# Ends of stages in a four-layer token kernel: two last blocks in turns, gathers under the softmax, experts in interleaved steps, stores by group

## The chip, the core and the metric

The kernel runs on one core of a Trainium2 chip. The core has a matrix engine (TensorE, "PE" in the profile, with its weight loads as "PEld"), a vector engine (VectorE, "DVE"), an activation engine (ScalarE, "ACT"), a general engine (GpSimd, "POOL"), an engine that mostly issues transfers (SyncE, "SP"), and 16 DMA engines. Each engine has a queue of its own and executes it in order; engines wait for each other through semaphores. ACT and POOL issue transfers too. The metric is the device time of one execution in microseconds (us); lower is better.

## What is computed

The input is eight images of 56 x 56 pixels with 128 channels. Four layers follow one another: a deformable convolution with an MLP, a whitening, and two token layers, in which an image is a list of 3136 tokens of 128 channels. Only the token layers matter here:

```python
t = t + attn(_ln_t(t))            # layer 2: softmax attention, 8 heads of 16
t = t + ffn(_ln_t(t))             # experts, below
t = t + linear_attn(_ln_t(t))     # layer 3: softmax(q), softmax(k), k^T v, norm
t = t + ffn(_ln_t(t))

logits = einsum('bsd,ed->bse', x, gate_w) + gate_b     # 64 experts
probs = softmax(logits, axis=1)                        # over the tokens
vals, idx = top_k(probs.transpose(0, 2, 1), 8)         # 8 tokens for each expert
pooled = einsum('bked,bke->bed', gathered, topv)       # weighted sum of the 8
h = gelu(einsum('ebd,edh->ebh', [pooled, 1], weight1)) # 512 hidden
out = einsum('ebh,eho->ebo', [h, 1], weight2)
outputs = zeros.at[idx].add(out * topv)                # back to the 8 tokens
```

Each expert chooses its eight tokens in an image by their gate logits, so an image's choice can be made only when all of its logits exist.

## The kernel before

The convolution and the whitening come first and are not touched. `token_layers` then runs these stages, one after another:

1. `attention_keys` normalises the tokens and makes the keys of all images.
2. `attend` is the softmax attention. Its scheduling is written out by hand: every engine runs its instructions in the order of the program. An image has two groups of four heads; a group has eight blocks of queries (384 wide, the last 448) and goes through the key tiles in steps. Scores are products on PE (L1252) into the bank pairs of pool `pss`, exponentials on ACT (L1260), 32 x 32 transposes on DVE (L1271) that let one exponential serve two pairs of blocks, moves of these squares by SP (L1287, twelve transfers a set) and POOL (L1298), and weighted sums on PE (L1305), added by DVE (L1324).
   A finished block goes through `finish`: divide by the sum (L1345 to L1353), load its tokens (L1359), project with p_o (L1366), add to the tokens (L1377), store them to `t_a` (L1378), statistics (L1382 to L1385, the power on POOL), normalise to `xn` (L1392), transpose on PE (p_tr, L1404), copy to `xT` (L1405), gate product (p_g, L1408), and write the logits `pr` (L1409). `finish` is a generator: at each `yield` the main loop takes back control and calls `go_on` once a step at most, the oldest block first. p_o, p_tr, p_g and the running sum `avx` share one bank (pool `psm`, tag `m`), so a `yield True` asks for a step at which that bank is free. When the loop has ended, the blocks that are left are finished one after another.
   After the last block of an image, `choose` (L1643 to L1707) takes the eight largest logits of each expert (MAX8, L1650) and their positions (FIND_INDEX8, L1653), the sum of exponentials (seven pieces on ACT, L1663), spreads positions and weights over 128 partitions by small products with an identity (p_take, L1679), gathers the tokens by indirect transfers of POOL (four, L1711), takes their statistics (L1697), normalises and weighs them and sums them to `pooled` (L1706).
3. `run_experts` makes the experts of layer 2. Two pieces of work alternate: `Spread.prepare` of each image (four gathers, and the matrix `s_w` that takes expert outputs back to tokens: `same` on DVE, L1757, added by POOL, L1767), and `Experts.run`, which goes through the 64 experts in 16 quarters of four. A quarter is: p_h (L1855 and bias L1859), gelu on ACT (L1861), transposes p_ht (L1864), copy to `hT` on DVE (L1868), p_o (L1872 and bias L1880), copy to `o` on DVE (L1883), four stores by ACT (L1887). Its weights, two transfers of 1 MB (L1823, L1826), are loaded four quarters ahead by SP; each quarter issues those of the quarter four later at its end. `Spread.run` then adds the result to the gathered tokens and scatters them back (32 indirect transfers, L1791).
4. `context_sums` makes k^T v of the linear attention.
5. `linear_layer` (L2064 to L2153) handles groups of 448 tokens, seven to an image. The groups run through `pipeline`, which starts one a turn and advances all that are in flight. The tokens of an image lie in one tile; each group adds its result to its part (POOL, L2129) and takes statistics. The last group of an image stores the whole image twice, to `t_c` and to the output (L2138), and goes on with `choose`.
6. `run_experts` again, with the weights of layer 3; its final scatter goes to the output.

Outside `attend` the order of instructions on each engine is decided by a scheduler at build time, from the dependencies and the program's order. Transfers that SP and ACT issue take eight semaphores in rotation, so each of them waits for the one eight places before it.

Of the kernel before, what the change touches and what calls it, by code (L numbers as in the profile page):

```python
# [19 lines left out]
T = 112  # L20
# [1134 lines left out]
def attend(tc, k, w, low, tok, kT_in, va_in, t_out, gate_w, gate_b, taken, pooled):  # L1155
# [11 lines left out]
    with ExitStack() as ctx:  # L1167
# [166 lines left out]

        def finish(n, g, b):
# [27 lines left out]
            p = psm.tile([128, KB + 1, C], F32, tag="m", name="p_o")  # L1363
# [9 lines left out]
            st = wp.tile([128, KB + 1, 6], F32, name="st")  # L1373
            mv = wp.tile([128, KB + 1, 2], F32, name="mv")
            rs = wp.tile([128, KB + 1], F32, name="rs")
# [14 lines left out]
            xn = wp.tile([128, KB + 1, C], F32, name="xn")  # L1390
            for i, (_, m) in enumerate(tiles):
                nc.vector.tensor_scalar(  # L1392
                    xn[:m, i],
                    t_sb[:m, i],
                    mv[:m, i, 0:1],
                    rs[:m, i : i + 1],
                    ALU.subtract,
                    ALU.mult,
                )
            yield True  # L1400
            xT = wp.tile([C, QB + 64], F32, name="xT")
            p = psm.tile([C, 512], F32, tag="m", name="p_tr")
            for i, (_, m) in enumerate(tiles):
                nc.tensor.transpose(p[:, 128 * i : 128 * i + m], xn[:m, i], k.ident[:m, :m])  # L1404
            nc.vector.tensor_copy(xT[:, :width], p[:, :width])  # L1405
            yield True
            p = psm.tile([E, 512], F32, tag="m", name="p_g")
# [15 lines left out]
        ready = []  # L1423
# [61 lines left out]
        for work in urgent:  # L1485
            go_on(work)
        while later:
            go_on(later[0])
# [156 lines left out]
def choose(nc, k, wp, ps, pr, t_in, taken, pooled):  # L1645
# [12 lines left out]
    nc.scalar.activation(found[:, 1], best, AF.Exp, bias=ntop)  # L1658
    yield
# [17 lines left out]
    p = ps.tile([128, 2, NC], F32, tag="m", name="p_take")  # L1677
    for j in range(TOP // NC):
        nc.tensor.matmul(  # L1679
            p[E * j : E * j + E],  # L1680
            k.ident[:E, :E],
            found[:, :, j :: TOP // NC],
            start=True,
            stop=True,
        )
    rows = wp.tile([128, NC], I32, name="rows")
    nc.vector.tensor_copy(rows, p[:, 0])
    nc.vector.tensor_copy(taken, p)
    x = wp.tile([128, NC, C], F32, name="chosen")
    for c in range(NC):  # L1690
        gather(nc, x[:, c], t_in, rows[:, c : c + 1])
    for _ in range(4):
        yield
# [107 lines left out]
class Experts:  # L1801

    def __init__(self, tc, pool, weight1, weight2, ahead):
        nc = tc.nc
        self.tc, self.pool = tc, pool
        self.weight1, self.weight2 = weight1, weight2
        self.loaded = [self.load(q) for q in range(ahead)]

        self.b1 = pool.tile([E, HID], F32, name="b1", bufs=1)
        nc.scalar.dma_start(self.b1, weight1[:, C, :])
        self.b2 = pool.tile([E, C], F32, name="b2", bufs=1)
        nc.scalar.dma_start(self.b2, weight2[:, HID, :])

        self.x = pool.tile([C, E, 32], F32, name="x", bufs=1)
        nc.gpsimd.memset(self.x, 0.0)

    def load(self, q):
        nc = self.tc.nc  # L1820
        es = slice(q * EG, (q + 1) * EG)
        w1 = self.pool.tile([C, EG, HID], F32, name="w1")
        nc.sync.dma_start(w1, self.weight1[es, :C, :].rearrange("e d h -> d e h"))  # L1823

        w2 = self.pool.tile([128, EG, 4 * C], F32, name="w2")
        nc.sync.dma_start(  # L1826
            w2, self.weight2[es, :HID, :].rearrange("e (p f) o -> p e (f o)", f=4)
        )
        return w1, w2

    def run(self, k, pooled, out):
# [4 lines left out]
        with ExitStack() as ctx:  # L1836
# [7 lines left out]
            loaded = list(self.loaded)  # L1844
            ahead = len(loaded)
            for q in range(n_q):
                w1, w2 = loaded[q]
                p = ps.tile([128, HID], F32, tag="h", name="p_h")
                rows = [p[32 * j : 32 * j + 32] for j in range(EG)]
                ones = [  # L1850
                    k.ident[:E, e : e + 1].to_broadcast([E, 32])
                    for e in range(q * EG, q * EG + EG)
                ]
                for j in range(EG):
                    nc.tensor.matmul(  # L1855
                        rows[j], x[:, q * EG + j], w1[:, j], start=True, stop=False
                    )
                for j in range(EG):
                    nc.tensor.matmul(rows[j], ones[j], self.b1, start=False, stop=True)  # L1859
                h = wp.tile([128, HID], F32, name="h")  # L1860
                nc.scalar.activation(h, p, AF.Gelu)  # L1861
# [6 lines left out]
                nc.vector.tensor_copy(hT, p)  # L1868
                p = ps.tile([128, C], F32, tag="o", name="p_o")
                for f in range(4):  # L1870
                    for j in range(EG):
# [3 lines left out]
                            w2[:, j, f * C : (f + 1) * C],  # L1875
# [3 lines left out]
                for j in range(EG):  # L1879
                    nc.tensor.matmul(  # L1880
                        p[32 * j : 32 * j + 32], ones[j], self.b2, start=False, stop=True
                    )
                nc.vector.tensor_copy(o[:, q], p)  # L1883
                if q + ahead < n_q:
                    loaded.append(self.load(q + ahead))
                for j in range(EG):
                    nc.scalar.dma_start(out[:, q * EG + j], o[32 * j : 32 * j + n_b, q])  # L1887
                yield
# [174 lines left out]
def linear_layer(tc, k, w, low, cw, t_in, xT_in, t_out, out, gate_w, gate_b, taken, pooled):  # L2063
# [5 lines left out]
    with ExitStack() as ctx:  # L2069
# [5 lines left out]
        def group(n, g):  # L2075
# [60 lines left out]
            if g == NG - 1:  # L2136
                for d in (t_out[n], out[n]):
                    nc.sync.dma_start(d.rearrange("(t p) c -> p t c", p=T), st_of[n][0])  # L2138
# [205 lines left out]
```

## Time and profile before

The median of three runs is 7727.34 us (7716.75 to 7728.98). The profile is that of one execution.

| | us |
|---|---|
| profiled execution | 7718.14 |
| its span, first to last instruction | 7716.3 |
| attention, end of its loop at about | 6500 |
| last logits of attention (end of the `pr` writes) | 6553.6 |
| first experts: first gather | 6582.2 |
| POOL's last addition to `s_w` there | 6655.9 |
| linear layer, about | 7033 to 7451 |
| its last `pooled` | 7481.8 |
| second experts: first gather | 7486.1 |
| final scatter | from 7626 on |

PE is busy 84% of the span, DVE 68%, ACT 54%, POOL 38%. These shares are averages over stages with different limits, so they must be read stage by stage. In a timeline row, the numbers are the start and the duration; then come the engine, the line, the operation, what it writes and reads, and in square brackets how long the engine had been idle and which instruction released it. The granted clock of PE is a share of full speed.

### The profile page before, as it was taken

What the parts mean: (1) busy time and instruction counts of PE and PEld (TensorE: products, weight loads), DVE (VectorE), ACT (ScalarE), POOL (GpSimd) and SP (SyncE); (2) the same over time, 40 slices, a digit from 0 to 9 for tenths busy, and PEclk for the clock granted to TensorE, in tenths of its full rate; (3) what the DMA queues carried; (4) which work ended last, traced back from release to release, by engine and by line L of the source; (5) the groups of instructions that cost most, each with busy time, mean ns of one, the idle gap of its engine ahead of it and who ended that gap; (6) DMA issues with size and microseconds to landing.
All of it is one profiled execution on the core that took longest, in us unless ns stands there. A gap on an engine that the chain in (4) does not pass through costs nothing. (4 is left out here: it accounts for less than half of the span.)

```text
span 7716.3 us, 157926 instructions
## 1 busy us (share of the span) xinstructions
PE 6482.3 (84%) x59883; PEld 2880.7 (37%) x59883; DVE 5284.8 (68%) x9856; ACT 4142.6 (54%) x6467; POOL 2935.1 (38%) x2555
## 2 busy tenths in 40 slices
PE   6659999556899999999999999999999997556654
PEld 4446666334233323323323323333333333245532
DVE  7975564366677777777777777777777776366752
ACT  4424444122666666666666666666666664056740
POOL 0011111022444444444444444444444443434653
PEclk8768898777999999999999999999999998788766
DMA  5453443376788778778778778778778775543543
GB/s 155 137 119 76 86 95 65 82 240 207 199 203 197 193 192 199 189 192 201 191 184 204 188 183 207 183 191 205 185 190 206 182 190 137 196 117 107 134 135 130
DMA packets 736303, 1287.38 MB, mean 167 GB/s; under 512 B 117698, under 2 KB 503108, under 8 KB 728516
## 3 DMA queue, kind: packets, MB, share of 16 engines
q1 hardware_dynamic: 725556, 1260.76, 65.1%
q0 software_dynamic: 6144, 12.60, 0.6%
q8 instruction: 484, 7.93, 0.5%
q10 hardware_dynamic: 3824, 3.68, 0.2%
q14 instruction: 295, 2.42, 0.1%
HBM read 286.04 MB, written 197.81 MB: 63 GB/s over the span
## 5 line engine op out<-in xcount | busy, mean ns | idle before, releaser
L1260 ACT ACTIVATE e<-p_s 128x768 f32<-128x768 f32 (+2 forms) x3712 | 2887.8, 830 | 1584.9 <-PE p_s L1252 1329.8
L1298 POOL COPY x<-sq 32x1152 f32<-32x1152 f32 x1792 | 2059.2, 1149 | 2067.6 <-PE p_s L1252 1330.0
L1271 DVE STREAM_TRANSPOSE sq<-e 128x768 f32<-128x768 f32 x2688 | 2434.5, 950 | 567.3 <-ACT e L1260 312.9
L1252 PE MATMUL p_s<-q,kT 32*128 32x384 f32 (+2 forms) x14848 | 1888.6, 548 | 33.6 <-ACT e L1260 18.6
L1305 PE MATMUL av<-e,va 128*32 128x384 f32 (+2 forms) x14848 | 1645.3, 515 | 30.4 <-DVE acc L1324 20.7
L1305 PE MATMUL avx<-x,va 128*32 128x384 f32 x10752 | 1138.3, 496 | 69.5 <-issue 40.2
L1252 PEld LDWEIGHTS p_s<-q,kT 32*128 32x128 f32 (+1 forms) x14848 | 654.8, 181 | 1252.6 <-issue 825.4
L1305 PEld LDWEIGHTS av<-e,va 128*32 128x32 f32 (+1 forms) x14848 | 294.5, 108 | 1049.4 <-issue 941.7
L1305 PEld LDWEIGHTS avx<-x,va 128*32 128x32 f32 x10752 | 353.2, 111 | 650.9 <-issue 595.2
L609 POOL TENSOR_TENSOR rs<-rs,mhalf 112x4 f32<-112x4 f32 x112 | 116.1, 1036 | 788.3 <-DVE rs L608 788.3
L1324 DVE TENSOR_TENSOR acc<-acc,avx 128x384 f32<-128x384 f32 x336 | 183.9, 547 | 229.9 <-PE avx L1305 228.6
L121 PE MATMUL p_tr<-ident,xn 112*128 112x112 f32 x672 | 134.6, 341 | 187.4 <-DVE xn L112 141.8
L1141 POOL TENSOR_TENSOR rs<-rs,mhalf 112x4 f32<-112x4 f32 (+2 forms) x136 | 168.1, 1236 | 269.3 <-DVE ntop L1942 123.8
L525 ACT COPY wT<-p_w 88x448 f32<-88x448 f32 x152 | 138.0, 922 | 194.1 <-PE p_w L523 161.4
L1990 ACT ACTIVATE xn<-t,ms,rs 112x128 f32<-112x128 f32 x448 | 185.3, 488 | 76.4 <-DVE ms L1983 76.4
L327 DVE SCALAR_TENSOR_TENSOR acc<-xp,dw,acc 128x3136 f32<-128x3136 f32 x56 | 194.3, 3478 | 31.3 <-ACT acc L322 31.2
L637 PE MATMUL p_f<-x1T,w 128*128 128x448 f32 x448 | 205.6, 583 | 4.4 <-DVE x1T L632 2.7
L121 PEld LDWEIGHTS p_tr<-ident,xn 112*128 112x128 f32 x672 | 98.7, 169 | 285.0 <-issue 185.1
L1385 POOL TENSOR_TENSOR rs<-rs,mhalf 128x3 f32<-128x3 f32 (+1 forms) x72 | 58.5, 815 | 365.0 <-DVE rs L1384 343.0
L523 PE MATMUL p_w<-ident,wide 112*88 112x112 f32 x896 | 146.5, 303 | 58.6 <-DMA px<-strips 34.1
L621 DVE TENSOR_TENSOR y<-y,p_rs 128x448 f32<-128x448 f32 x112 | 69.3, 619 | 176.6 <-PE p_rs L614 176.6
L122 ACT COPY xT<-p_tr 128x448 f32<-128x448 f32 x112 | 59.6, 532 | 229.8 <-PE p_tr L121 203.7
(354 smaller groups left out, 7830.9 us busy)
## 6 DMA issues: line engine op xcount, KB each, us to landing
x<-sq SPq DMA_DIRECT2D x5376, 144.0 KB
w<-in_L_ffn_weight_dram SPq DMA_DIRECT2D x64, 1024.0 KB
px<-strips SPq DMA_DIRECT2D x64, 616.0 KB
va_d<-va SPq DMA_DIRECT2D x16, 1600.0 KB
xT_d<-xT SPq DMA_DIRECT2D x112, 224.0 KB
xT<-xT_d SPq DMA_DIRECT2D x112, 224.0 KB
kT_d<-kT SPq DMA_DIRECT2D x16, 1568.0 KB
t<-t_a SPq DMA_DIRECT2D x16, 1568.0 KB
```

Source lines behind the costliest of these rows:

```text
L121: nc.tensor.transpose(p[:, i, :], src[:, i, :], k.ident[:T, :T])
L327: nc.vector.scalar_tensor_tensor(acc, xp[:, j // 3 : j // 3 + IH, j % 3 : j % 3 + IW], dw[:, j : j + 1], acc, ALU.mult, ALU.add,)
L523: nc.tensor.transpose(p[:, g], around[:, :, g], k.ident[:T, :T])
L637: nc.tensor.matmul(p, q.w1[:, f * 128 : (f + 1) * 128], x1T, start=True, stop=True)
L1141: nc.gpsimd.tensor_tensor(rs, rs, k.mhalf[:m, :n], ALU.pow)
L1252: nc.tensor.matmul(ss[j // 2][:m, j % 2, :width], kT[rows, 128 * i : 128 * i + m], q[rows, :width], start=True, stop=True,)
L1260: nc.scalar.activation(e[:m, 2 * j : 2 * j + 2, :width], ss[j][:m, :, :width], AF.Exp)
L1271: nc.vector.transpose(sq[:, :, i, j : j + 2].rearrange("p s j c -> p j s c"), exps[u, b, a, i][:, j : j + 2, :QB].rearrange("p j (s c) -> ...
L1298: nc.gpsimd.tensor_copy(*moves.pop(0))
L1305: nc.tensor.matmul(out, keys[u, b][1][:m, i, j, :], e[j], start=start, stop=stop)
L1324: nc.vector.tensor_tensor(to, to, in_order(av), ALU.add)
L1990: nc.scalar.activation(out[:, i], x[:, i], AF.Identity, bias=ms[:, i : i + 1], scale=rs[:, i : i + 1])
```

## The change

Six edits, all around the ends of stages:

- In `finish`, once the main loop is over (`ending`), p_o, p_tr and p_g take their banks from the score pool (three buffers) and not from the single bank, and the blocks that are left are advanced two at a time in turns. `st`, `mv`, `rs` and `xT` get two buffers, and the normalised tokens are written into `t_sb` itself; the tile `xn` is gone. This last part holds in the main loop too.
- In `choose`, the positions are spread and the tokens gathered directly after FIND_INDEX8; the exponentials follow, and then the weights are spread by a second set of small products. There are fewer `yield`s between the gathers and the statistics. `choose` is used by `attend` and by `linear_layer`.
- In `Experts`, a quarter is cut into `first` (p_h, gelu), `second` (p_ht, hT) and `third` (p_o, o, stores), and the program runs second(q-1), first(q), third(q-1).
- The copy to `hT` is on ACT.
- The load of the first weights of a later quarter is issued in `first`, that of the second weights in `third`.
- In `linear_layer`, each group stores its own 448 tokens to `t_c` and to the output.

```diff
--- before.py
+++ after.py
@@ -1332,6 +1332,15 @@
                 urgent.append(work)
                 later.append(work)
 
+        def bank(shape):
+
+            if not ending:
+                return psm.tile(shape, F32, tag="m", name="p_m")
+            p = pss.tile([128, 2, 512], F32, name="p_s")[: shape[0], 0]
+            if len(shape) == 3:
+                p = p.rearrange("p (a c) -> p a c", c=shape[2])
+            return p
+
         def finish(n, g, b):
 
 
@@ -1360,7 +1369,7 @@
                     t_sb[:m, i], tok[n][s].rearrange("(t p) c -> p t c", p=m)
                 )
             yield True
-            p = psm.tile([128, KB + 1, C], F32, tag="m", name="p_o")
+            p = bank([128, KB + 1, C])
             for i, (t, m) in enumerate(tiles):
                 for h in range(2):
                     nc.tensor.matmul(
@@ -1370,9 +1379,9 @@
                         start=(h == 0),
                         stop=(h == 1),
                     )
-            st = wp.tile([128, KB + 1, 6], F32, name="st")
-            mv = wp.tile([128, KB + 1, 2], F32, name="mv")
-            rs = wp.tile([128, KB + 1], F32, name="rs")
+            st = wp.tile([128, KB + 1, 6], F32, name="st", bufs=2)
+            mv = wp.tile([128, KB + 1, 2], F32, name="mv", bufs=2)
+            rs = wp.tile([128, KB + 1], F32, name="rs_b", bufs=2)
             for m, i, s in spans:
                 nc.vector.tensor_tensor(t_sb[:m, i], t_sb[:m, i], p[:m, i], ALU.add)
                 nc.sync.dma_start(
@@ -1387,10 +1396,9 @@
                 )
             yield False
             yield False
-            xn = wp.tile([128, KB + 1, C], F32, name="xn")
             for i, (_, m) in enumerate(tiles):
                 nc.vector.tensor_scalar(
-                    xn[:m, i],
+                    t_sb[:m, i],
                     t_sb[:m, i],
                     mv[:m, i, 0:1],
                     rs[:m, i : i + 1],
@@ -1398,13 +1406,13 @@
                     ALU.mult,
                 )
             yield True
-            xT = wp.tile([C, QB + 64], F32, name="xT")
-            p = psm.tile([C, 512], F32, tag="m", name="p_tr")
+            xT = wp.tile([C, QB + 64], F32, name="xT", bufs=2)
+            p = bank([C, 512])
             for i, (_, m) in enumerate(tiles):
-                nc.tensor.transpose(p[:, 128 * i : 128 * i + m], xn[:m, i], k.ident[:m, :m])
+                nc.tensor.transpose(p[:, 128 * i : 128 * i + m], t_sb[:m, i], k.ident[:m, :m])
             nc.vector.tensor_copy(xT[:, :width], p[:, :width])
             yield True
-            p = psm.tile([E, 512], F32, tag="m", name="p_g")
+            p = bank([E, 512])
             nc.tensor.matmul(p[:, :width], gate_w, xT[:, :width], start=True, stop=True)
             nc.vector.tensor_scalar(
                 pr[:, first : first + width], p[:, :width], gate_b, None, ALU.add
@@ -1420,7 +1428,7 @@
             except StopIteration:
                 later.remove(work)
 
-        ready = []
+        ready, ending = [], False
         loads = [(u, b) for u in range(1, len(parts)) for b in (8, 7, 3, 2, 1, 6, 5, 4, 0)]
 
         def reload():
@@ -1484,8 +1492,10 @@
             from_squares()
         for work in urgent:
             go_on(work)
+        ending = True
         while later:
-            go_on(later[0])
+            for work in later[:2]:
+                go_on(work)
 
 
 def attend_any(tc, k, w, yv, kT_in, va_in, t_out, gate_w, gate_b, taken, pooled, t_g):
@@ -1656,6 +1666,27 @@
     found = wp.tile([E, 2, TOP], F32, name="found")
     nc.vector.tensor_copy(found[:, 0], at)
     nc.scalar.activation(found[:, 1], best, AF.Exp, bias=ntop)
+
+    def spread(i):
+
+        p = ps.tile([128, NC], F32, tag="m", name="p_take")
+        for j in range(TOP // NC):
+            nc.tensor.matmul(
+                p[E * j : E * j + E],
+                k.ident[:E, :E],
+                found[:, i, j :: TOP // NC],
+                start=True,
+                stop=True,
+            )
+        nc.vector.tensor_copy(taken[:, i], p)
+
+    yield True
+    spread(0)
+    rows = wp.tile([128, NC], I32, name="rows")
+    nc.vector.tensor_copy(rows, taken[:, 0])
+    x = wp.tile([128, NC, C], F32, name="chosen")
+    for c in range(NC):
+        gather(nc, x[:, c], t_in, rows[:, c : c + 1])
     yield
     part = wp.tile([E, NG], F32, name="part")
     for g in range(NG):
@@ -1674,23 +1705,8 @@
     nc.vector.reciprocal(tot, tot)
     nc.vector.tensor_scalar(found[:, 1], found[:, 1], tot, None, ALU.mult)
     yield True
-    p = ps.tile([128, 2, NC], F32, tag="m", name="p_take")
-    for j in range(TOP // NC):
-        nc.tensor.matmul(
-            p[E * j : E * j + E],
-            k.ident[:E, :E],
-            found[:, :, j :: TOP // NC],
-            start=True,
-            stop=True,
-        )
-    rows = wp.tile([128, NC], I32, name="rows")
-    nc.vector.tensor_copy(rows, p[:, 0])
-    nc.vector.tensor_copy(taken, p)
-    x = wp.tile([128, NC, C], F32, name="chosen")
-    for c in range(NC):
-        gather(nc, x[:, c], t_in, rows[:, c : c + 1])
-    for _ in range(4):
-        yield
+    spread(1)
+    yield
     st = wp.tile([128, NC, 6], F32, name="cst")
     mv = wp.tile([128, NC, 2], F32, name="cmv")
     for c in range(NC):
@@ -1802,11 +1818,12 @@
...
     def __init__(self, tc, pool, weight1, weight2, ahead):
         nc = tc.nc
         self.tc, self.pool = tc, pool
         self.weight1, self.weight2 = weight1, weight2
-        self.loaded = [self.load(q) for q in range(ahead)]
+        self.loaded = [(self.load_first(q), self.load_second(q)) for q in range(ahead)]
 
         self.b1 = pool.tile([E, HID], F32, name="b1", bufs=1)
         nc.scalar.dma_start(self.b1, weight1[:, C, :])
@@ -1816,17 +1833,20 @@
         self.x = pool.tile([C, E, 32], F32, name="x", bufs=1)
         nc.gpsimd.memset(self.x, 0.0)
 
-    def load(self, q):
-        nc = self.tc.nc
+    def load_first(self, q):
         es = slice(q * EG, (q + 1) * EG)
         w1 = self.pool.tile([C, EG, HID], F32, name="w1")
-        nc.sync.dma_start(w1, self.weight1[es, :C, :].rearrange("e d h -> d e h"))
+        self.tc.nc.sync.dma_start(w1, self.weight1[es, :C, :].rearrange("e d h -> d e h"))
+        return w1
+
+    def load_second(self, q):
+        es = slice(q * EG, (q + 1) * EG)
 
         w2 = self.pool.tile([128, EG, 4 * C], F32, name="w2")
-        nc.sync.dma_start(
+        self.tc.nc.sync.dma_start(
             w2, self.weight2[es, :HID, :].rearrange("e (p f) o -> p e (f o)", f=4)
         )
-        return w1, w2
+        return w2
 
     def run(self, k, pooled, out):
 
@@ -1841,50 +1861,74 @@
             x = self.x
             nc.vector.tensor_copy(x[:, :, :n_b], pooled.rearrange("c n e -> c e n"))
             o = cp.tile([128, n_q, C], F32, name="o")
-            loaded = list(self.loaded)
-            ahead = len(loaded)
-            for q in range(n_q):
-                w1, w2 = loaded[q]
+            w1s, w2s = (list(s) for s in zip(*self.loaded))
+            ahead = len(w1s)
+            hs = {}
+
...
+            def first(q):
+
                 p = ps.tile([128, HID], F32, tag="h", name="p_h")
                 rows = [p[32 * j : 32 * j + 32] for j in range(EG)]
...
                 for j in range(EG):
                     nc.tensor.matmul(
-                        rows[j], x[:, q * EG + j], w1[:, j], start=True, stop=False
+                        rows[j], x[:, q * EG + j], w1s[q][:, j], start=True, stop=False
                     )
                 for j in range(EG):
-                    nc.tensor.matmul(rows[j], ones[j], self.b1, start=False, stop=True)
-                h = wp.tile([128, HID], F32, name="h")
-                nc.scalar.activation(h, p, AF.Gelu)
...
+                if q + ahead < n_q:
+                    w1s.append(self.load_first(q + ahead))
+                hs[q] = wp.tile([128, HID], F32, name="h")
+                nc.scalar.activation(hs[q], p, AF.Gelu)
+
+            def second(q):
+                h = hs.pop(q)
                 p = ps.tile([128, 4, EG, 32], F32, tag="t", name="p_ht")
                 for f in range(4):
                     nc.tensor.transpose(
                         p[:, f].rearrange("p j b -> p (j b)"), h[:, f::4], k.ident
                     )
                 hT = wp.tile([128, 4, EG, 32], F32, name="hT")
-                nc.vector.tensor_copy(hT, p)
+                nc.scalar.copy(hT, p)
+                return hT
+
+            def third(q, hT):
                 p = ps.tile([128, C], F32, tag="o", name="p_o")
                 for f in range(4):
                     for j in range(EG):
                         nc.tensor.matmul(
                             p[32 * j : 32 * j + 32],
                             hT[:, f, j],
-                            w2[:, j, f * C : (f + 1) * C],
+                            w2s[q][:, j, f * C : (f + 1) * C],
                             start=(f == 0),
                             stop=False,
                         )
...
                 nc.vector.tensor_copy(o[:, q], p)
                 if q + ahead < n_q:
-                    loaded.append(self.load(q + ahead))
+                    w2s.append(self.load_second(q + ahead))
                 for j in range(EG):
                     nc.scalar.dma_start(out[:, q * EG + j], o[32 * j : 32 * j + n_b, q])
+
+            hT = None
+            for q in range(n_q + 1):
+                if q:
+                    hT = second(q - 1)
+                if q < n_q:
+                    first(q)
+                if q:
+                    third(q - 1, hT)
                 yield
 
 
@@ -2133,9 +2177,9 @@
             ms = minus_mean(nc, wp, rs, mv)
             xn = wp.tile([T, GT, C], F32, name="xn")
             scale_shift(nc, xn, t, rs, ms)
-            if g == NG - 1:
-                for d in (t_out[n], out[n]):
-                    nc.sync.dma_start(d.rearrange("(t p) c -> p t c", p=T), st_of[n][0])
+            for d in (t_out[n], out[n]):
+                d = d.rearrange("(t p) c -> p t c", p=T)
+                nc.sync.dma_start(d[:, g * GT : (g + 1) * GT], t)
             yield
             nT = wp.tile([C, QC], F32, name="nT")
             transpose_group(nc, k, ps, "m", nT, xn, nc.scalar.copy)
```

More of the change, by code (lines that the diff above doesn't have):

```diff
@@ L1843, in run, with ones @@
             o = cp.tile([128, n_q, C], F32, name="o")
-            loaded = list(self.loaded)
-            ahead = len(loaded)
-            for q in range(n_q):
-                w1, w2 = loaded[q]
+            w1s, w2s = (list(s) for s in zip(*self.loaded))
+            ahead = len(w1s)
+            hs = {}
+            def ones(e):
+                return k.ident[:E, e : e + 1].to_broadcast([E, 32])
+            def first(q):
                 p = ps.tile([128, HID], F32, tag="h", name="p_h")
                 rows = [p[32 * j : 32 * j + 32] for j in range(EG)]
[L1850 to L1853, printed above, removed]
                 for j in range(EG):
                     nc.tensor.matmul(
-                        rows[j], x[:, q * EG + j], w1[:, j], start=True, stop=False
+                        rows[j], x[:, q * EG + j], w1s[q][:, j], start=True, stop=False
                     )
                 for j in range(EG):
-                    nc.tensor.matmul(rows[j], ones[j], self.b1, start=False, stop=True)
-                h = wp.tile([128, HID], F32, name="h")
-                nc.scalar.activation(h, p, AF.Gelu)
+                    nc.tensor.matmul(
+                        rows[j], ones(q * EG + j), self.b1, start=False, stop=True
+                    )
+                if q + ahead < n_q:
[4 more added lines that the diff above has]
+                h = hs.pop(q)
                 p = ps.tile([128, 4, EG, 32], F32, tag="t", name="p_ht")
@@ L1880, in run @@
                     nc.tensor.matmul(
-                        p[32 * j : 32 * j + 32], ones[j], self.b2, start=False, stop=True
+                        p[32 * j : 32 * j + 32],
+                        ones(q * EG + j),
+                        self.b2,
+                        start=False,
+                        stop=True,
                     )
```

## The prediction

> **What bounds the kernel now.** I read the busy shares by stage first: us, then busy time and count of PE, PEld, DVE, ACT, POOL, then granted clock, DMA share and GB/s.
>
> ```profile
> 2230.00:6500.00 4270.00, 4108.67 (x39025) 1354.36 (x39018) 3223.90 (x4665) 2733.09 (x3578) 2018.81 (x1782) 0.98 0.80 193
> 6500.00:6580.00 80.00, 26.68 (x89) 17.02 (x88) 35.65 (x100) 5.52 (x15) 10.11 (x11) 0.53 0.09 26
> 6580.00:6656.00 76.00, 48.23 (x332) 17.62 (x332) 38.43 (x68) 4.27 (x6) 63.35 (x57) 0.67 0.71 238
> 6656.00:6732.00 76.00, 55.37 (x644) 24.02 (x644) 10.82 (x22) 6.57 (x11) 0.00 (x0) 0.80 0.69 240
> 7033.00:7451.00 418.00, 280.51 (x1532) 204.82 (x1532) 303.98 (x1112) 297.16 (x1001) 273.75 (x258) 0.78 0.51 130
> 7451.00:7485.00 34.00, 4.33 (x20) 3.89 (x20) 14.49 (x40) 5.06 (x16) 5.93 (x6) 0.50 0.54 196
> ```
>
> The attention loop (first row) is TensorE's: 4109 of 4270 us busy. The change touches it only a little; its aim is the rows below, where no engine is busy half the time (second and sixth) or one engine leads: POOL in the third row (the first experts, while `Spread.prepare` runs), nothing in the fourth (the rest of them). In the linear layer DVE, ACT and POOL are each busy some 70% and no single one bounds.
>
> The end of attention is a chain. The timeline of DVE (start, duration, line, operation; in brackets the idle time before it) for one of the five last blocks:
>
> ```profile
> 6515.16 0.56 DVE L1377 TENSOR_TENSOR t<-t,p_o 128x384 f32<-128x384 f32 x1 [3.02 <-PE p_o L1366]
> ...
> 6518.28 0.86 DVE L1392 TENSOR_SCALAR xn<-t,mv,rs 128x128 f32<-128x128 f32 x3 [1.03 <-POOL rs L1385]
> 6519.70 0.56 DVE L1405 COPY xT<-p_tr 128x384 f32<-128x384 f32 x1 [0.57 <-PE p_tr L1404]
> 6521.90 0.61 DVE L1409 TENSOR_SCALAR pr<-p_g,gate_b 64x384 f32<-64x384 f32 x1 [1.64 <-PE p_g L1408]
> 6525.52 0.56 DVE L1377 TENSOR_TENSOR t<-t,p_o 128x384 f32<-128x384 f32 x1 [3.02 <-PE p_o L1366]
> ```
>
> The period is 6525.52 − 6515.16 = 10.36 us, of which DVE works about 4; the next block's p_o (2.93 us on PE) starts only behind this one's `pr`, since all four products share one PSUM bank. Then follows `choose`, also a chain:
>
> ```profile
> 6557.19 3.41 DVE L1653 FIND_INDEX8 at<-best,pr 64x8 uint32<-64x3136 f32 x1
> ...
> 6566.43 0.15 DVE L1673 TENSOR_REDUCE tot<-part 64x1 f32<-64x7 f32 x1 [5.63 <-ACT every L1663]
> ...
> 6570.65 0.29 DVE L1697 BATCH_NORM_STATS2 cst<-chosen 128x6 f32<-128x128 f32 x1 [2.90 <-DMA chosen<-t_a,rows]
> ```
>
> The indices are known at 6560.8, but the gathers wait until 6567.96 for a softmax sum that they don't use. Last, DVE's waits in the attention loop (total, times, longest):
>
> ```profile
> DVE sq L1271 <- DMA x<-sq: 164.4, 95, 4.5
> ...
> DVE sq L1271 <- DMA t_a<-t: 7.2, 10, 1.4
> ```
>
> **What the Trainium skill says.** "DMA: Bandwidth & Descriptors", Anatomy of one DMA: a fixed cost near 2.0 us, mostly the receipt of the write. The trace agrees where the queues are quiet (the first gather of `choose`, 6567.96, is read at 6570.65), and not inside the attention loop, where kT loads take 2.5/5.0/8.0 us to land (least, median, most). The same page, Specifications, has 358 GB/s of HBM per core; the trace's busiest stretches of weight loads show 331 to 372, so it agrees. "TensorE: Matmul & The Clock Gate", Part 1: the clock halves after an idle window. The trace agrees: granted 0.53 and 0.50 in the two drained rows, and in the expert stage the p_o products of one quarter take 1.08 us or, cold, 1.94.
>
> **Part by part.** Sums are against the profiled execution: 7718.1 us, span 7716.3; the median of the runs shown is 7727.3, 9 above it.
>
> *Two blocks in turns.* With the score banks used when the loop has ended, a pair runs as: p_o A 0 to 2.9, p_o B to 5.9; DVE A's add and statistics (2.1) to 5.1; B's to 8.0; normalise A (.86) to 8.9; PE transposes A (.90) to 9.9; copy (.56) to 10.5; p_g A (1.54) to 12.1; B's transposes to 13.0, copy 13.6, p_g 15.2. So about 15.0 to 15.2 a pair against 20.7. Five blocks are two pairs and one alone: −11.5. Bounds −3 (if the token load of the second of a pair, queued on SP behind the store of the first, is late by 4 us each time) and −13.
>
> *Gather under the softmax.* FIND ends 6560.6; cast .2, two small products and copies 1.1 (the p_take row of today: .38 on PE, then .3 on DVE): gathers at 6562.2 in place of 6567.96. Four of them at 1.26, then the landing: last one at 6568.5. But DVE does the four statistics only behind `tot` and the second spread (6567.7), .5 each: 6569.7, against 6574.8 now. −5 (bounds −3, −6).
>
> *In the loop.* (a) Each of seven images has four more small products on TensorE, .2 us each, and one more step that wants the free bank: +6 in all. (b) The normalisation now writes into `t`, which the store to t_a is reading, so DVE waits for that store. Between the store's issue on SP and the normalisation I measure, block by block, over 9.5 us in 41 blocks but 2.5 to 5.0 us in 23, where SP was issuing 12 square moves of .6 us first. The trace has no landing of these stores; the row of like size is the kT load, 5.0 median and 8.0 most, the quiet value is 2.4. At 5.0 DVE waits some 1.5 us in 23 blocks, 35 us. What is queued behind are the square transposes of the next key tile, then ACT's exponentials, then PE. But DVE waits 164 us for moves today and PE idles 161 us in the whole loop for all reasons, so I let a fifth through: +7. Bounds 0 (landing 2.4) and +100 (landing 8, all passed on). Together +13.
>
> *Experts, first time.* Up to 6656 POOL bounds: 32 gathers of 1.26 and 24 additions of 1.28, 71 us, not touched. Then quarters come every 6.8 us (p_o at 6678.3, 6685.6, 6691.3): p_h 2.1, gelu wait .8, p_ht .75, hT wait .8, p_o 1.5 at full clock, 5.8; up to 7.3 cold. With hT on ACT and p_o one step late, only the gelu wait stays: 5.15 at full clock. Loads bound it: 2.1 MB a quarter is 5.6 to 6.3 us at 331 to 372 GB/s. ACT now has hT behind its oe issues (four, 1.3 to 1.5 us, longer when they wait for a load's semaphore), so I take 6.0. But DVE's o copies stay behind `prepare`, so only four quarters, not five, are done when POOL ends. From POOL's end (6655.9) to the last issue (6730.1) it is 74.2 now; then it is 2.3 to the first step, ten steps of 6.0 and a last one of 3.1 that starts no new quarter, 65.4: −9 (bounds 0 at 6.9, −15 at 5.4).
>
> *Experts, second time.* Today the copy of `pooled` into x stands on DVE behind two index casts that wait for gathers' landings (3.44 and 4.81 us), 7498.2; it moves ahead of them, to about 7489.7. POOL is idle 10 us between 7542 and 7563, waiting for DVE's `same`; that goes, so POOL ends 72 after its start, not 83. Experts end at about 115 after the first gather in place of 131: −15 (bounds 0, −20).
>
> *Linear layer.* Stores: 16 of 1.6 MB, each 4.5 to 5 us of SP's time, become 112 of 224 KB at .32, ahead of token loads that are two turns (15 us) early: nothing, hidden by that lead; without it +2 a turn. `choose` of image n now issues its gathers right behind FIND; POOL stands up to 3 us for it, then 5 us for four gathers, while the next groups' rs powers wait. Today it is so too, only later: DVE's longest wait for POOL's rs is 5.6, once an image. So 0, bounds ±20.
>
> *End of the linear layer.* Today MAX8 of the last image starts at 7457.2 although `pr` is ready at 7451.2: in front of it on DVE are the statistics of the previous image, whose gathers were issued at 7445.9, and landed 6.9 us later among an output store and 6.3 MB of weights (DMA share 1.00 in 7440 to 7460). Choosing earlier takes these away, 6, and the softmax another 5: −11 (bounds −5, −13).
>
> The final scatter (32 by 2.5 us in turn) is as it was. Sum: −11.5 − 5 + 13 − 9 − 15 + 0 − 11 = −38.5. 7727 − 39 is 7688; the profiled execution would be near 7680.
>
> **Rivals.**
> 1. *The store holds up DVE* (other side). Place: the normalisation in the attention loop. If stores land at 7 us and PE feels all of it, 23 blocks lose 3.5 each, 80 us in place of 7: 7761. It decides from about 2.9 us a block fully passed on. For it: PE is 96% busy and nothing refills a gap; against: ten waits for that very store today, longest 1.4, and DVE has a fifth of its time free. 7 in 100.
> 2. *The linear layer gets slower*: POOL's gathers, now tied to FIND, hold up rs and t of three groups in flight by 3.5 us an image, eight times: +28, 7716. For it: three engines at 70% each, so an order decides. 13 in 100.
> 3. *The linear layer gets faster*: the gathers fall into POOL's idle stretch, and the 5.2 us stall of DVE goes seven times: −36, 7652. 17 in 100.
> 4. *The experts gain nothing*, their period stays that of the loads (6.8 is 310 GB/s) or of oe issues that hold up hT: +24, 7712. 11 in 100.
> 5. My forecast, 7688, own range 7668 to 7708: 52 in 100.
>
> **How the numbers follow.** Half of rival 1 (above 7722) and most of 3's lower half (below 7648) are left out: 7648 to 7722. A measurement can't tell 0.2% (15.5 us) from nothing: faster is below 7712: all of forecast and 3, half of 4, a third of 2, some 0.78. Within 0.2%: the rest of 2 and 4, 0.14. Slower: rival 1 and a little of 2, 0.08.
>
> **What would show it.** The last blocks' additions (L1377's) in pairs 15 us apart; gathers of the last attention image 1.6 us behind FIND; waits of DVE's normalisation for t_a under 50 us in sum, and the attention loop within 15 us of 4270; expert quarters every 6 us; x copied 4 us into the second experts' stage; 51 us an image in the linear layer; MAX8 of its last image straight behind `pr`. I am wrong if the loop grows by 50, or the linear layer moves by 20 either way.

## The result, and the profile after

The changed kernel takes 7655.5 us (median of four, 7648.9 to 7657.9) where the kernel before took 7725.7 in the runs beside it (four, 7716.8 to 7729.0): a ratio of 0.991, 95% interval 0.9892 to 0.9927. Later, on the same chip as nine runs of the kernel before (median 7715.2), it took 7653.2: 0.992, 0.9908 to 0.9935. So it gains 62 to 70 us. The forecast was 39, 7688, with a range of 7648 to 7722.

The gain can be followed from stage to stage in the two profiles (7718.1 and 7657.9 us; spans 7716.3 and 7656.2). Each row is the time between two points that both traces have.

| stretch | before | after | difference | forecast |
|---|---|---|---|---|
| attention loop, first to last score product | 4523.7 | 4528.0 | +4.3 | +13 |
| drain: first addition of the last blocks to last logits | 48.8 | 37.6 | −11.2 | −11.5 |
| last logits of attention to `pooled` | 25.5 | 20.0 | −5.5 | −5 |
| first experts, first gather to last copy of o | 146.3 | 133.8 | −12.5 | −9 |
| linear layer, first q exponential to last logits | 404.7 | 395.8 | −8.9 | 0 |
| last logits there to last `pooled` | 30.6 | 21.2 | −9.4 | −11 |
| second experts, first gather to last copy of o | 129.5 | 111.9 | −17.6 | −15 |

They sum to −60.8, with −38.5 forecast; the spans differ by 60.1. The busy shares by stage in the profile after, in the columns of the prediction (stretch, PE, PEld, DVE, ACT, POOL, granted clock, DMA share, GB/s):

```profile
6487.00:6570.00 83.00, 35.80 (x175) 19.54 (x167) 42.88 (x116) 8.30 (x18) 15.80 (x15) 0.63 0.25 64
6570.00:6642.00 72.00, 40.38 (x296) 14.87 (x296) 36.01 (x62) 6.41 (x11) 62.88 (x56) 0.74 0.63 217
6642.00:6706.00 64.00, 46.13 (x682) 21.27 (x681) 3.50 (x12) 12.41 (x21) 0.00 (x0) 0.97 0.87 316
6657.00:6698.00 41.00, 29.20 (x420) 13.11 (x420) 2.04 (x7) 8.23 (x14) 0.00 (x0) 1.00 1.01 369
7022.00:7373.00 351.00, 251.96 (x1457) 190.41 (x1455) 274.87 (x1020) 270.71 (x920) 251.14 (x237) 0.82 0.53 137
```

The third row is the one to look at: behind POOL's work in the first experts the granted clock is 0.97, not 0.80, and the DMA engines carry 316 GB/s, not 240. The fourth row is the middle of the third: for 41 us the DMA engines are busy without a break and carry 369 GB/s. The stage has come to its loads. PE's waits in this stretch say the same (total, times, longest). The kernel before, where no wait is for weights:

```profile
PE p_o L1872 <- DVE hT L1868: 8.6, 11, 0.8
PE p_ht L1864 <- ACT h L1861: 8.6, 11, 0.8
```

The changed kernel:

```profile
PE p_ht L1892 <- ACT h L1886: 7.8, 10, 0.8
PE p_h L1876 <- DMA w<-in_L_ffn_weight_dram: 6.0, 7, 1.5
PE p_o L1903 <- DMA w<-in_L_ffn_weight_dram: 2.2, 3, 1.6
```

The last blocks of attention, the timeline of DVE in the changed kernel (start, duration; in brackets the idle time before it and who ended it):

```profile
6509.48 0.52 DVE L1386 TENSOR_TENSOR t<-t,p_s 128x384 f32<-128x384 f32 x1
...
6513.13 0.56 DVE L1386 TENSOR_TENSOR t<-t,p_s 128x384 f32<-128x384 f32 x1 [1.60 <-DMA t<-tok]
...
6518.76 0.61 DVE L1417 TENSOR_SCALAR pr<-p_s,gate_b 64x384 f32<-64x384 f32 x1 [0.87 <-PE p_s L1416]
...
6521.78 0.61 DVE L1417 TENSOR_SCALAR pr<-p_s,gate_b 64x384 f32<-64x384 f32 x1 [1.63 <-PE p_s L1416]
6524.64 0.56 DVE L1386 TENSOR_TENSOR t<-t,p_s 128x384 f32<-128x384 f32 x1 [2.25 <-PE p_s L1375]
```

A pair takes 6524.64 − 6509.48 = 15.16 us; the working gave 15.0 to 15.2. The second addition waits 1.6 us for its tokens, whose load SP issues behind the first block's store: the wait that the lower bound of that step named, at its small end.

`choose`, on POOL: the gathers follow 1.3 us behind the indices (cast at 6554.10), and no longer the softmax (`tot` at 6559.90).

```profile
6555.40 1.06 POOL L1727 DMA_INDIRECT chosen<-t_a,rows  x1 [12.57 <-DVE rows L1686]
...
6563.11 1.04 POOL L1141 TENSOR_TENSOR rs<-rs,mhalf 128x4 f32<-128x4 f32 x1 [2.91 <-DVE rs L1140]
```

The power stood at 6575.16 in the profile before, 21.5 behind the last logits; now it is 16.0 behind them.

A quarter of the experts, from the timeline of PE in the first experts:

```profile
6647.85 0.75 PE L1892 MATMUL p_ht<-ident,h 128*128 128x128 f32 x4 [0.78 <-ACT h L1886]
...
6648.53 1.08 PE L1903 MATMUL p_o<-w,hT 128*32 128x128 f32 x32
...
6649.90 1.06 PE L1876 MATMUL p_h<-w,x 128*32 128x512 f32 x8
...
6652.73 0.75 PE L1892 MATMUL p_ht<-ident,h 128*128 128x128 f32 x4 [0.78 <-ACT h L1886]
...
6661.18 1.06 PE L1876 MATMUL p_h<-w,x 128*32 128x512 f32 x8 [1.46 <-DMA w<-in_L_ffn_weight_dram]
```

From one p_ht to the next it is 4.88 us; the only wait left in this quarter is that for gelu, 0.78. Two quarters later the products wait for weights instead.

### The profile page after: what moved, and what is told of

It is laid out like the page before. It is cut to its first block, busy times and chain, and to the rows that moved or that the text cites. A ratio compares the mean times of both kernels' runs of the same rounds, so it can differ in the third digit from the quotient of the medians.

```text
span 7656.2 us, 158331 instructions
## 1 busy us (share of the span) xinstructions
PE 6459.4 (84%) x59947; PEld 2867.8 (37%) x59947; DVE 5281.9 (69%) x9840; ACT 4163.3 (54%) x6499; POOL 2939.2 (38%) x2555
## 5 line engine op out<-in xcount | busy, mean ns | idle before, releaser
L1394 POOL TENSOR_TENSOR rs_b<-rs_b,mhalf 128x3 f32<-128x3 f32 (+1 forms) x72 | 58.5, 815 | 356.5 <-DVE rs_b L1393 347.0
```

## The experiments

Times are those of single stretches of one profile, as in the table above, unless a median is given.

**The order of choose alone.**

```diff
+    yield True
+    spread(0)          # positions only
+    ... gather x4
     yield
     part = ...         # exponentials, tot
     yield True
-    p_take, rows, gather x4; four yields
+    spread(1)          # weights
+    yield
```

> The kernel before with the new order of choose alone. Before: last score product ends at 6483.0, last logits 6553.6, pooled of the last attention image 6579.1 (25.5 after the logits); linear layer from its first q exponential (7046.5) to its last (7408.3) 361.8; from there to the last pooled 73.5. After: 6487.5; 20.0 after the logits; 351.1; 66.0. Theory A (the loop grew by 4.5 because of choose: its last step, normalise and p_pool, now stands behind a block's divide on DVE, and PE waits 33.9 for it in place of 14.6): last score at 6487 to 6488. Rival (the loop grew because the normalisation is in place): 6483 within 1. Theory B (the linear layer gained by choose): body 351 to 353, end 66 to 68. Rival B (by the stores): body 361 to 363.

Measured: the attention loop 4513.0 (score products end 6479.8, begin 1966.3); the last logits to `pooled` 20.1; the linear layer's first to last q 357.4; from there to the last `pooled` 65.6. The last score product is earlier than both ranges. Theory A falls all the same: PE waits just as long at p_pool (33.6) as in the changed kernel, and the loop is the shortest of all. Theory B and its rival both miss: on the measure named beforehand, first to last q, choose gives 4.4 of the changed kernel's 10.7. From the first q to the last logits, as in the table above, it takes 398.7 (before 404.7, changed kernel 395.8), so 6.0 of 8.9. Up to the last MAX8 it takes 400.2 (before 410.7, changed kernel 397.2), but 4.6 of these 10.5 belong to the end of the stage, where MAX8 follows the logits sooner. Three kernels further down keep the linear layer and the choose of the kernel before; they take 360.1 to 361.4 from first to last q and 403.1 to 404.1 to the last logits, so the gain is clear of that spread. What choose does there is seen in DVE's waits over the stretch from the first to the last q (total, times, longest; `y` waits for the power of the first statistics of a group, `ms` for that of the second). The kernel before:

```profile
DVE y L2126 <- POOL rs L2123: 62.3, 37, 5.6
```

With the order of choose alone:

```profile
DVE y L2132 <- POOL rs L2129: 42.4, 38, 1.4
...
DVE ms L1989 <- POOL rs L1141: 13.9, 6, 5.0
```

The long stall, once an image, behind the four gathers on POOL is gone from `y` (the three kernels just named still have it, 5.6 to 5.7). Part of it comes back as a stall of `ms`, 5.0 in one image and some 1.8 in each of the others, and 6 us of 62 are left as gain in these two rows. An image now takes 49.3 us from one MAX8 to the next (before 50.7).

**Stores by group alone.**

```diff
-            if g == NG - 1:
-                for d in (t_out[n], out[n]): store of the image
+            for d in (t_out[n], out[n]): store of the group
```

> The kernel before with the stores of the linear layer cut by group, nothing else. Attention and first experts as before (last score 6483 within 1). Theory B (the linear layer's body gained by choose): body 361 to 363, not shorter; its end perhaps 1 to 5 shorter, since the last image's store is small when the gathers are issued. Rival B: body 351 to 353.

Measured: first to last q 357.6; first q to the last logits 401.2, to the last MAX8 405.7; from that MAX8 to `pooled` 24.6, as before. So it lies between the theories: 4.2 of 10.7 from first to last q, 3.5 of 8.9 to the last logits. The last score product ends at 6476.3 and the first experts take 148.1, though nothing before the linear layer was edited: single profiles move by that much. DVE's waits are those of before (62.7 for the power, longest 5.7). PE is busy 242 us in place of 253 with the same products, at a granted clock of 0.84 in place of 0.81; but the kernel with hT on ACT alone, further down, shows 244 us at 0.83 and still takes 360.4, so that doesn't bring the gain. The 357.6 is 2.5 below the shortest of the four profiles with the linear layer of before (360.1 to 361.8). The stores seem to give something; by what wait isn't shown, and it is one profile. The two experiments together give 9.5 to the last logits against the 8.9 of the changed kernel.

**Normalised tokens in a tile of their own again**, in the changed kernel.

```diff
-                    t_sb[:m, i],
+                    xn[:m, i],              # xn: one buffer; xT: one buffer
                     t_sb[:m, i],
```

> The changed kernel with the normalised tokens in a tile of their own again (one buffer, and one buffer for the transposed ones, so that it fits). Theory A: the last score product still ends at 6487 to 6488, waits of DVE's normalisation for the store vanish (0.5 in sum before), and the last blocks still come in pairs 15.1 apart. Rival: 6483 within 1, and the sum of the run 4 to 5 lower.

Measured: score products end at 6488.8 (begin 1960.5; 4527.8), pairs 15.0 apart (6510.62, 6525.62), 7662.0 us. The loop didn't get shorter, but a loop alone can't decide this: that of one and the same program moves by 6 between two profiles, as is shown below. What speaks against the rival is the wait itself. In the changed kernel it is this row of DVE's waits in the loop, two waits out of 67 stores:

```profile
DVE t L1400 <- DMA t_a<-t: 0.5, 2, 0.3
```

With `xn` kept, the row is gone. With `xn` and `xT` both single the turns are not slower, so the second buffer of `xT` buys nothing here.

**One more turn ahead of p_pool**, in the changed kernel.

```diff
     rs = rsqrt(nc, k, wp, mv, NC)
-    yield True
+    yield
     ... normalise
+    yield True
     p = ps.tile([C, E], F32, tag="m", name="p_pool")
```

> The changed kernel with one more turn given up in choose between the power and the normalisation, and the bank asked for only ahead of p_pool, so that TensorE comes to p_pool a step after DVE was given the normalisation. Theory A: PE's waits for DVE at p_pool inside the attention loop (33.9 us, 14) fall below 5, and the last score product ends 15 to 30 earlier, 6457 to 6472; the run takes 7625 to 7645. Rival (what PE loses there it makes up by the scores already queued, so that the loop is bound elsewhere): last score 6483 to 6488, 7650 to 7658.

Measured: 7646.3 us (four, 7642.4 to 7650.0), 0.9908 of the kernel before (0.9891 to 0.9924): not to be told from the changed kernel's own ratio. The loop takes 4518.3. PE's waits in the loop, the changed kernel:

```profile
PE p_pool L1722 <- DVE chosen L112: 33.9, 14, 4.3
...
PE av L1305 <- DVE acc L1324: 4.2, 8, 0.7
```

and with one more turn, where p_pool has left the list:

```profile
PE av L1305 <- DVE acc L1324: 32.6, 15, 4.1
```

The last score product ends at 6479.5, earlier than the rival's range and later than theory A's. Theory A is refuted: the wait did not go, it changed its name. In the timeline of both kernels DVE has the same lump of work once an image in front of it (a block's division and this normalisation behind it, 4 to 6 us), and the next product of PE waits for it, whichever that is: these two rows sum to 35 us in the kernel before (14.6 and 20.7), 38 in the changed one, 33 here. PE's idle time in the loop is 159 us before, 158 in the changed kernel, 153 with choose alone, 157 here.

**The edits to the experts alone.**

```diff
+            for q in range(n_q + 1):
+                if q: hT = second(q - 1)      # p_ht, hT on ACT
+                if q < n_q: first(q)          # p_h, gelu, load of w1
+                if q: third(q - 1, hT)        # p_o, o, stores, load of w2
```

> The kernel before with the edits to the experts alone (first, second and third in turns, hT on ACT, loads split). From the first gather of the stage to the last copy of o: before 146.3 in the first experts and 129.5 in the second; changed kernel 133.8 and 111.9; with choose alone 151.4 and 122.4. Theory C (the first experts gain by the edits to them, the second by these and by the copy of pooled that stands ahead since choose was reordered): first 134 to 137, second 116 to 121, with x copied about 12 into the stage as before. Rival (the edits to the experts also move the copy of pooled forward): second 111 to 114, x copied within 4. Rival (choose did all): 146 to 151 and 126 to 130.

Measured: first experts 139.6, second 114.6, x copied 12.0 into the second stage. The size in the first is a miss: 3 over the range. In the second, the time lies between the two ranges, just above the rival's, and without the rival's cause, since x was copied as late as before. So the early copy of x is worth little once quarters run in turns: with it, the five kernels with all edits and hT on ACT took 111.9, 113.9, 112.7, 115.7 and 113.5.

**hT on ACT alone.**

```diff
-                nc.vector.tensor_copy(hT, p)
+                nc.scalar.copy(hT, p)
```

> The kernel before with the copy to hT on ACT and nothing else. Theory C: the chain inside a quarter is as long as before, so the later quarters still come every 6.5 to 7.3; only what stood behind the prepare work on DVE gains: first experts 141 to 147, second 120 to 128. Rival (the gain of the experts is that hT left DVE): 133 to 138 and 111 to 118.

Measured: 146.7 and 122.6, as theory C has it: nothing in the first experts, 4 to 7 in the second. The later quarters of the first experts come 6.1 to 7.6 apart, and the products of p_o take 417 ns in the median, as in the kernel before (420); with quarters in turns they take 273.

**Quarters in turns, hT on DVE.** The edits to the experts alone, with the line just shown undone.

> The changed edits to the experts alone, but with the copy to hT left on DVE. Theory C: the later quarters come every 5.2 to 6.1 since the chain is broken, but hT stands behind the prepare work on DVE while POOL is busy: first experts 135 to 142, second 115 to 124. Rival (the steps in turns give nothing without ACT): 144 to 151 and 122 to 130.

Measured: 129.9 and 114.8, shorter in the first experts than with hT on ACT (139.6 there), and below the range of both theories. Turns are the cause of the gain, and the move of hT takes some of it back there. The split of the loads came with the turns and wasn't tried by itself; but PE waits for no weights in this stretch of the kernel before, so it can't have been what held PE up there. In this kernel PE's waits for hT behind POOL's work are gone as well.

**The last five blocks three and two in turns**, in the changed kernel.

```diff
-            for work in later[:2]:
+            for work in later[:3]:      # t, st, mv, rs: three buffers, xT: one
```

> The changed kernel with the last five blocks of attention taken three and two in turns in place of two, two and one (three buffers for the tokens and the statistics, one for the transposed tokens, so that it fits). From the first of their additions to the last logits: before 48.8, changed kernel 37.6. Theory D (the turns fill the waits of the chain: three blocks take about 19, two 15): 32 to 34, and the run takes 4 to 5 less than the changed kernel. Rival (SP's loads of tokens, each behind the store before it, hold up the third block): 36 to 39.

Measured: 30.1 from the first addition to the last logits, better than the 32 to 34 of theory D; 7652.8 us (four, 7636.0 to 7660.1), 0.9913 (0.9889 to 0.9936), from which a gain of 7 can't be read.

**The changed kernel once more.** No edit.

> The changed kernel once more, for what one profile of it varies by. The loop of attention, from its first to its last score product, was 4523.7 before and 4528.0 in the changed kernel; runs with its order of choose gave 4513 to 4528 (idle of TensorE there 153 to 160 in all). Theory E (the 4.3 is variation between executions): the loop differs from 4528 by 3 or more in this profile or the stages before the loop by 3 or more, idle of TensorE 153 to 160; drain 37.6, first experts 134 to 137, second 111 to 114 again. Rival (the loop really grew): 4527 to 4529.

Measured: the loop 4521.9, drain 37.7, first experts 133.6, second 113.5; 7653.2 us (five). Theory E holds: the loop of the same program moved by 6.1 between two profiles, the short stretches by 0.1 to 1.6. So a difference of 4 in one loop can't be read.

**Three and two in turns, hT on DVE.**

> The changed kernel with the last blocks three and two in turns, and the copy to hT on DVE again. Drain from the first addition to the last logits 30 (37.6 in the changed kernel). Theory F (hT belongs on DVE: o is copied earlier in the first experts): first experts 128 to 131, second 112 to 116; in all 9 to 13 less than the changed kernel. Rival (the 129.9 of the run with hT on DVE was luck with its weight loads): first experts 133 to 137, second 111 to 116; 5 to 9 less.

Measured: drain 27.7, first experts 127.8, second 114.2; 7647.6 us (five, 7637.8 to 7651.0), 0.9911 of the kernel before (0.9898 to 0.9925), 5.6 below the changed kernel in the same comparison (7653.2, five). Theory F holds for the stage: two kernels with turns and hT on DVE took 129.9 and 127.8, six with hT on ACT 133.6 to 139.6. The whole is short of 9 to 13 and lies in the rival's 5 to 9, and the intervals of the two overlap, so a gain over the changed kernel isn't shown. In the one profile (7650.0) the loop of attention was long (4531.8), 4 to 10 over the changed kernel's; the loops of the other four executions aren't known. The drain:

```profile
6515.07 0.52 DVE L1386 TENSOR_TENSOR t<-t,p_s 128x384 f32<-128x384 f32 x1
6517.03 0.56 DVE L1386 TENSOR_TENSOR t<-t,p_s 128x384 f32<-128x384 f32 x1
6520.83 0.55 DVE L1386 TENSOR_TENSOR t<-t,p_s 128x384 f32<-128x384 f32 x1 [1.71 <-DMA t<-tok]
...
6531.88 0.55 DVE L1386 TENSOR_TENSOR t<-t,p_s 128x384 f32<-128x384 f32 x1 [0.93 <-PE p_s L1375]
6533.88 0.55 DVE L1386 TENSOR_TENSOR t<-t,p_s 128x384 f32<-128x384 f32 x1
```

Three blocks take 16.8 us, and the two behind them 10.9 to the last logits. What is left of waiting is SP's load again, 1.71.

## Why the prediction was right, and where it was not

The sign, and every stage that should gain, came as forecast; the size was too small by 23 to 31 us of 62 to 70. The result lies outside the prediction's own range of 7668 to 7708, and within 7648 to 7722 only because that range took in a part of rival 3 as well. It lies near rival 3's 7652, but by luck: the −36 of that rival didn't come. Step by step:

*Two blocks in turns*: right in mechanism and size, 15.16 a pair, −11.2 against −11.5.

*Gather under the softmax*: right, 20.0 from logits to `pooled`. The gathers start 1.3 behind the cast (1.6 forecast), and DVE's statistics stand behind `tot` as worked out.

*In the loop*, +13: wrong. The term (b), 7 us for DVE's wait for the store, took 5.0 us for the landing of the store, read as the median of the kT loads. That reading was wrong, and so was the statement that the trace has no landing of the stores. In the semaphore records of the profile before, the 67 stores of the loop land 1.8/2.4/4.1 us behind their issue (least, median, most), and 143 kT loads 2.5/2.8/5.6. So the quiet value of 2.4, the lower bound of the term, was the right one in the busy loop too, and the fixed cost near 2.0 us that the prediction set aside for the loop is close to what the trace shows there. The normalisation comes 3.0 us behind the store's issue at the earliest (2.6 in the changed kernel), and DVE waited 0.5 us in all, twice. The term (a), 6 us for small products, can't be seen: kernels with the loop of before took 4523.7, 4522.3, 4526.0, 4534.5 and 4522.4, those with the new order of choose (the one with one more turn left aside) 4528.0, 4513.0, 4527.8, 4526.6, 4521.9 and 4531.8; the means are 4525.8 and 4524.9. The +4.3 in the table is such variation. The window named "attention loop" in the prediction began 271 us inside the loop, which changes none of its steps. Rival 1 rested on the same landing and is out with it.

*Experts, first time*: −12.5 to −9, right in mechanism. As worked out, four quarters are done when POOL ends, which is at 71.4. In the profile before POOL ended at 73.6; five other kernels with the same work on POOL show 71.5 to 72.1, so some 2 of the 12.5 are variation. Behind POOL's end the stage is 10.3 shorter. The mis-sized term is the steps: from the fifth copy of o to the last, eleven steps take 59.4, 5.4 each, where ten of 6.0 and a last one of 3.1 were forecast; the last one wasn't short. The load bound, 5.6 to 6.3 a quarter, was right where it applied: 2.1 MB at 369 GB/s are 5.7, and the seven steps between 6657.6 and 6698.9 take 5.9 each. The steps before them, with weights in hand, take 4.9 to 6.4. The 369 is above the 358 GB/s that the prediction named as a core's share; here the measurement decides. Rival 4 falls: the period didn't stay at 6.8, and PE has no wait for hT there.

*Experts, second time*: −17.6 to −15, right in size, partly for another reason. I gave the copy of x a large share; it moved ahead as forecast (1.5 us into the stage) but is worth some 1 us beside turns, which is within the spread (114.6 without, 113.5 in the mean of five with it). It seems to be worth more where quarters still run as a chain: with choose alone 122.4, where two kernels with the late copy took 129.5 and 126.4. POOL ends 75.2 after its start, not 72.

*Linear layer*, 0 with bounds of 20: this is the other step that failed. I wrote that DVE's longest wait for the power, 5.6 an image, would stay, "only later". It became 1.4, and an image 49.0 us in place of 50.7. Rival 3 named the direction (DVE's stall goes) and put it at −36; the gain is −8.9, since POOL's four gathers still take 5 us and the stall partly moves to another power, that of the second statistics (13.9). The experiment with choose alone shows this for about two thirds of the gain to the last logits (less than half of that to the last q); for the part with the stores no cause is shown. Rival 2, which had the same gathers hold up the groups, is seen in that 13.9, but what is lost there is less than what `y` gains.

*End of the linear layer*: −9.4 to −11. MAX8 starts 1.4 behind the last logits (6.0 before), since the choice of the image before isn't wholly out of the way; the softmax gives 4.8.

So two terms of the sum account for most of the 22 us that the two profiles differ from the forecast: the loop, 9 too much (13 if its +4.3 is variation), and the linear layer, 9 too little.

## What to carry to other kernels

At the end of a stage, look for chains in which every engine waits: running two or three instances in turns costs little more than buffers, and its gain can be added up from one period of the chain. Here two in turns came out within 0.3 us, three in turns 2 to 4 better than worked out. A broken chain can gain twice: TensorE's granted clock was higher with quarters in turns, too. Estimate the new period at full clock and then check it against the loads, which is where this one ended. A wait in a list is a symptom: taking away the instruction that waits (p_pool) moves the wait to the next in line when the engine that is late stays late. So compare an engine's idle time in sum as well as row by row.

## What I had not expected of the hardware

Between POOL's last addition and the last copy of o in the first experts, the clock granted to TensorE was 0.70, 0.76, 0.82 and 0.82 in the four kernels whose quarters run as a chain, and 0.88 to 1.00 in the eight with quarters in turns. The p_o products of the stage took 417 to 421 ns in the median in the chains and 273 in turns: the same products, a third shorter. Much of what single profiles of the chain differ by goes with this: the stage took 146.3 and 146.7 at 0.82, 148.1 at 0.76 and 151.4 at 0.70.

Why the clock is lower in the chain isn't shown. In its records it is either 1.0 or 0.5, for stretches of about 3.4 us or a multiple of it. PE's busy share doesn't tell the two apart: 76% of this stretch in the kernel before and 74% in the changed one. In turns PE gets through more products in the time (684 in 62.6 us, 644 in 72.9), but that can be the effect as well as the cause. Nor does the longest gap tell them apart: it was 0.8 us in the kernel before, at 0.82, and 1.6 in the changed kernel, at 0.97. So the cold p_o products of this stage, which the prediction set beside an idle window, are not explained by one.

The copy to hT takes 586 ns on ACT and 692 on DVE, yet the stage as a whole is 4 to 12 us longer with it on ACT; of the kernels at a granted clock of 0.97, 133.8 on ACT and 129.9 on DVE, it is 4. With hT on ACT, o of the third quarter is copied 56 us into the stage and not 40 to 42, and one quarter fewer is done when POOL ends. That fits 4 us, but it is an order that the scheduler chose; why it did so, and whether another order would take the difference away, was not tried.
